# A first block convolved in pieces beside its own scans, inputs held whole, and a load of 97 rows split in two

## The chip, the cores and the metric

The kernel runs on one core of one Trainium2 chip. The metric is device time in microseconds: the median of several executions. Beside it stands one profiled execution, taken by the hardware profiler, with its own time and the span from its first to its last instruction. A core has five engines, each with its own queue of instructions that it works off in order: PE (TensorE, matmuls; PEld is its weight load), DVE (VectorE), ACT (ScalarE), POOL (GpSimd) and SP (SyncE), which here issues every DMA. Data lies in DRAM, in SBUF (on chip, up to 128 partitions) or in PSUM (where matmuls write).

## The reference

The program is a network of four layers on four images of 96 channels and 64x64 pixels, all in float32. Layers 0 and 1 are of concern here.

Layer 0 takes an image as a sequence of 4096 tokens and passes it twice through a Mamba block. Its core:

```
h  = layernorm(seq);  xs, z = split(h @ in_w)
xc = silu(depthwise conv of 4 taps over xs)
dt, B, C = split(xc @ xproj_w);  delta = softplus(dt @ dt_w + dt_b)
state[t] = exp(delta[t]*A) * state[t-1] + delta[t]*B[t]*xc[t]      # 16 states per channel
y  = sum over states of state*C + D*xc;   seq += (y*silu(z)) @ out_w
```

It ends in a 1x1 convolution and a batch norm over all four images (so nothing of the next layer can begin before the last image is done), and adds the input: `x0 = bn(out) + x`.

Layer 1 normalizes x0 in groups of three channels over the image, and passes it through two "ss2d" blocks, then adds x0 again. A block's core:

```
xa, z = split(x @ in_w);   xc = silu(depthwise conv 3x3 over xa)
for d in 4 directions (rows, columns, and both reversed):
    delta, B, C from tokens of xc in that direction;   scan as above, 8 states per channel
    ysum += y + D*xc, put back in row order
out = (layernorm(ysum) * silu(z)) @ out_w
```

Layers 2 and 3 (a Fourier mixer, attention and two feed-forward parts) follow and are not touched.

## The kernel before

The program has three stages, one after the other: `stage_mamba` (layer 0), `stage_ss2d` (layer 1) and `stage_tokens` (layers 2 and 3).

**How a scan is laid out.** Tokens are taken in turns of T=1024. For a turn the channels, spread over their states, fill the 128 partitions of a *unit*: 8 channels by 16 states in layer 0 (24 units a turn), 16 channels by 8 states in layer 1 (6 units a turn). The helper class `Scan` runs the units. For each it loads delta (`sc_d`, read from a DRAM copy `dd` so that each channel's row is repeated for its states), ACT makes exp(delta*A), DVE runs the scan (`TENSOR_TENSOR_SCAN`), POOL multiplies by C (`sc_h`), and PE sums over the states into `y`. For two units in three the input delta*x is spread by PE into PSUM (`s`) and multiplied by B on DVE; for the third it is loaded from DRAM (`sc_u`) and multiplied on POOL. Three units of layer 1 are reduced together, a *round*.

**What a turn needs first.** In layer 1 `Tokens.prepare` makes delta from xc by PE (`wdt`), ACT (bias, Softplus) and stores it as `dd`; `narrow` splits the B and C rows into bfloat16 parts (`bc_in`, `bc_part`, `bcd`, `bc_stack`), and `mix` spreads them over the partitions by PE (`selbc`) into `bc`.

**Blocks.** Layer 1 has eight blocks in the order image 0, image 1 (first pass), image 0, image 1 (second pass), then images 2 and 3 likewise. A block is 4 directions by 4 turns by 6 units, 96 units. `Block.prepare` runs `first_input` if it is a first pass, then the convolution (8 pieces of 8 rows, each 9 matmuls over the padded image `xp` into PSUM, an eviction on ACT into `xc`, and a Silu every 32 rows), then the gates (8 matmuls `w_in`, evicted into `ysum`, a Silu every 32 rows, stored to DRAM as `szd`). `ysum` later takes the sums of the scans. `xc` and `ysum` have two buffers each, so blocks alternate; `xp` has one. `first_input` loads the stage's input `mid` and the image `x` in pieces of 512 pixels into small buffers of a ring of two, scales `mid` by the batch norm (ACT), adds `x` (POOL), takes statistics (DVE) and stores the piece to DRAM as `x0d`; after the group statistics it loads every piece back from `x0d` and ACT writes it, scaled, into `xp`. `Block.finish` normalizes, multiplies by the gate and projects, into `xp` for the second pass, or adds `x0d` and stores.

**What sets the order.** Both scan stages are recorded first and placed afterwards. The class `Plan` records every operation with what it depends on; `Plan.order` then places them, each engine taking the earliest recorded operation that its own cost figures say is ready (the PSUM tiles named `mm`, two of them, are given out in the same pass). All of these have the line number of the one call that emits them, L467. What was recorded earlier goes first when both are ready. The order of recording is set by `Scan.run`: at each unit s it loads ahead (LOOK = 5 units), and lets `Work` objects take steps. A `Work` is a generator with a number of steps and a unit by which it is due; `pace` takes steps in proportion, `finish` takes the rest at once. `plan(s)` hands them in: the turn's `ready` (prepare), `narrowed` and `mixed`, and `between[n]` beside block n: the finish of block n-1 and the preparation of block n+1. Before the first unit, the first block's preparation is finished whole, turns 0 and 1 are prepared and narrowed, and turn 0 is mixed.

**The start of the first stage.** Before recording, `stage_mamba` loads its weights. `w_conv0`, the taps of the convolution, is 97 rows (96 channels and one for the bias of the norm) of 1536 numbers, repeated in each row. DVE multiplies it with the projection that PE has put in PSUM into `conv_w` (L799), copies the gate's part (`z_w`, L800), and so frees the two PSUM tiles that the first LayerNorm uses next.

Of the kernel before, what the change touches and what calls it, by code (L numbers as in the profile page):

```python
# [11 lines left out]
F32 = mybir.dt.float32  # L12
# [737 lines left out]
def stage_mamba(ctx: ExitStack, k: Common, x: bass.AP, mid: bass.AP, bn: bass.AP):  # L750
# [33 lines left out]
    dp_q = wp.tile([CP, 2, 64], F32, name="dp_q")  # L784
    with tc.tile_pool(name="m_ld", bufs=1) as ld:
        in_w = k.load(ld, "w_in0")
        taps = k.load(ld, "w_conv0")
        gl = ld.tile([C, C + 1], F32, name="gl")
        for i in range(2):
            nc.vector.tensor_scalar(dp_p[:, i, :], k.ident, vec("Dp", i, 0), None, ALU.mult)  # L790
            for h in range(2):
                g = slice(64 * h, 64 * h + 64)
                nc.vector.tensor_scalar(dp_q[g, i, :], k.ident[g, g], vec("Dp", i, 1)[g, :], None, ALU.mult)
            nc.vector.tensor_scalar(gl[:, 0:C], k.ident[:C, :C], k.vec("ln_g", i), None, ALU.mult)
            nc.vector.tensor_copy(gl[:, C:C + 1], k.vec("ln_b", i))
            pw = ps.tile([C + 1, 2 * DIN], F32, tag="mm", name="in_ps")
            nc.tensor.matmul(pw, gl, in_w[:, i, :], start=True, stop=True)
            for tap in range(4):
                nc.vector.tensor_tensor(conv_w[:, i, tap, :], pw[:, 0:DIN], taps[:, i, tap, :], ALU.mult)  # L799
            nc.vector.tensor_copy(z_w[:, i, :], pw[:, DIN:2 * DIN])  # L800
# [236 lines left out]
def stage_ss2d(ctx: ExitStack, k: Common, x: bass.AP, mid: bass.AP, bn: bass.AP, mid2: bass.AP):  # L1037
# [63 lines left out]
    class Block:  # L1101


        def __init__(self, b, i):
            self.b, self.i = b, i
            self.ready = None

        def first_input(self):

            b = self.b  # L1110
            st = wk.tile([C, L // W, 6], F32, tag="gn_st", name="gn_st", bufs=1)
            for t in range(L // W):
                cs = slice(t * W, (t + 1) * W)
                x0 = wk.tile([C, W], F32, tag="x0", name="x0")
                nc.sync.dma_start(out=x0, in_=mid[b, :, cs])
                xr = wk.tile([C, W], F32, tag="xr", name="xr")
                nc.sync.dma_start(out=xr, in_=x[b, :, cs])
                yield
                nc.scalar.activation(x0, x0, AF.Identity, scale=bn[:, 0:1], bias=bn[:, 1:2])
                nc.gpsimd.tensor_tensor(x0, x0, xr, ALU.add)  # L1120
                yield
                nc.vector.bn_stats(st[:, t, :], x0)
                nc.sync.dma_start(out=x0d[b, :, cs], in_=x0)
            mv = wk.tile([C, 2], F32, tag="gn_mv", name="gn_mv")
            nc.vector.bn_aggr(mv, st.rearrange("p a b -> p (a b)"))
            gm_ps = ps.tile([C, 1], F32, tag="mm", name="gm_ps")
            nc.tensor.matmul(gm_ps, group, mv[:, 0:1], start=True, stop=True)
            gm = wk.tile([C, 1], F32, tag="gm", name="gm")
            nc.vector.tensor_copy(gm, gm_ps)
            dm = wk.tile([C, 1], F32, tag="dm", name="dm")  # L1130
            nc.vector.tensor_tensor(dm, mv[:, 0:1], gm, ALU.subtract)
            gq = wk.tile([C, 1], F32, tag="gq", name="gq")
            nc.vector.scalar_tensor_tensor(gq, dm, dm, mv[:, 1:2], ALU.mult, ALU.add)
            yield
            gv_ps = ps.tile([C, 1], F32, tag="mm", name="gv_ps")
            nc.tensor.matmul(gv_ps, group, gq, start=True, stop=True)
            grs = k.rsqrt(wk, gv_ps, EPS, "gn_rs")
            yield
            shift = wk.tile([C, 1], F32, tag="gn_sh", name="gn_sh")
            nc.vector.scalar_tensor_tensor(shift, gm, -1.0, grs, ALU.mult, ALU.mult)  # L1140
            for t in range(L // W):
                x0 = wk.tile([C, W], F32, tag="x0", name="x0")
                nc.sync.dma_start(out=x0, in_=x0d[b, :, t * W:(t + 1) * W])
                yield
                nc.scalar.activation(
                    rows(8 * t, 8), x0.rearrange("p (h w) -> p h w", w=HW), AF.Identity, scale=grs, bias=shift
                )

        def prepare(self):
            i = self.i  # L1150
            if i == 0:
                yield from self.first_input()
            xc = self.xc = big.tile([C, L], F32, tag="xc", name="xc")
            for r in range(0, HW, 8):
                pa = ps.tile([C, W], F32, tag="mm", name="xc_ps")
                for tap in range(9):
                    nc.tensor.matmul(
                        pa, conv_w[:, i, tap, :], xp[:, r + tap // 3:r + tap // 3 + 8, tap % 3:tap % 3 + HW],
                        start=tap == 0, stop=tap == 8,
                    )  # L1160
                nc.scalar.activation(xc[:, r * HW:(r + 8) * HW], pa, AF.Identity, bias=k.vec("s_conv_b", i))
                yield 4
                if r % 32 == 24:
                    cs = slice((r - 24) * HW, (r + 8) * HW)
                    nc.scalar.activation(xc[:, cs], xc[:, cs], AF.Silu)

            ysum = self.ysum = big.tile([C, L], F32, tag="ysum", name="ysum")
            self.szd = dr.tile([C, L], F32, tag="szd", name="szd")
            for r in range(0, HW, 8):
                pz = ps.tile([C, W], F32, tag="mm", name="z_ps")  # L1170
                nc.tensor.matmul(pz, in_w[:, i, C:2 * C], rows(r, 8), start=True, stop=True)
                nc.scalar.copy(ysum[:, r * HW:(r + 8) * HW], pz)
                yield
                if r % 32 == 24:
                    cs = slice((r - 24) * HW, (r + 8) * HW)
                    nc.scalar.activation(ysum[:, cs], ysum[:, cs], AF.Silu)
                    nc.sync.dma_start(out=self.szd[:, cs], in_=ysum[:, cs])
# [24 lines left out]
    class Tokens(Turn):  # L1202
# [32 lines left out]
        def prepare(self):  # L1235

            i, d = self.block.i, self.d
            self.block.ready.finish()
            xt = self.xt = self.tokens()
            delta = wk.tile([CD, T], F32, tag="delta", name="delta", bufs=1)  # L1240
            for at in range(0, T, W):
                pd = ps.tile([CD, W], F32, tag="mm", name="dt_ps")
                nc.tensor.matmul(pd, wdt[:, i, d, :], xt[:, at:at + W], start=True, stop=True)
                bias = dt_b[:, i * NDIR + d:i * NDIR + d + 1]
                nc.scalar.activation(delta[:, at:at + W], pd, AF.Identity, bias=bias)
            nc.scalar.activation(delta[0:C, :], delta[0:C, :], AF.Softplus)
            dd = dr.tile([CD, T], F32, tag="dd", name="dd", bufs=2 + 2)
            nc.sync.dma_start(out=dd, in_=delta)
            yield
            du = wk.tile([C, T], F32, tag="du", name="du", bufs=2)  # L1250
            nc.gpsimd.tensor_tensor(du, delta[0:C, :], xt, ALU.mult)
            ud = dr.tile([C, T], F32, tag="ud", name="ud", bufs=2 + 1)

            nc.sync.dma_start(out=ud[64:C, :], in_=du[64:C, :])
            self.dd, self.du, self.ud = dd, du, ud
# [52 lines left out]
    for n in range(len(blocks)):  # L1308
        steps, count = [], 0
        if n > 0:  # L1310
            steps.append(blocks[n - 1].finish())
            count += 33
        if n + 1 < len(blocks):
            steps.append(blocks[n + 1].prepare())
            count += 9 + 8 * 4 + 26 * (1 - blocks[n + 1].i)
        between.append(Work(chain(*steps), count, (n + 1) * slot - 2 - 6 * 2))
        if n + 1 < len(blocks):
            blocks[n + 1].ready = between[-1]
    blocks[0].ready = Work(blocks[0].prepare(), 80, 0)

    def plan(s):
        out = []
        n, at = divmod(s, size)
        if at == 3 and 1 <= n + 1 < len(turns):
            turns[n + 1].mixed.due = s + 3
            out.append(turns[n + 1].mixed)
        if at == 5 and 2 <= n + 2 < len(turns):
            turns[n + 2].narrowed.due = s + 3
            out.append(turns[n + 2].narrowed)
        if at == 2 and 2 <= n + 2 < len(turns):  # L1330
            turns[n + 2].ready.due = s + 3
            out.append(turns[n + 2].ready)
        n, at = divmod(s, slot)
        if at == 6 and n < len(blocks):
            out.append(between[n])
        return out

    blocks[0].ready.finish()
    for turn in turns[0:2]:
        turn.ready.finish()  # L1340
        turn.narrowed.finish()
    turns[0].mixed.finish()
    sc.run(units, plan)
    for _ in blocks[-1].finish():
# [318 lines left out]
```

## Time and profile before

| | us |
|---|---|
| median of 3 runs | 7759.35 (7758.62 to 7760.86) |
| profiled execution, its own time | 7736.41 |
| its span | 7734.3 |
| PE busy | 6714.1 (87%) |
| DVE busy | 5775.7 (75%) |
| POOL busy | 5765.4 (75%) |
| ACT busy | 4616.8 (60%) |
| DMA queue of SP | 68.5% of 16 engines, 1368.76 MB |

The first stage lasts until about 2910 us, the second until about 6420, the third to the end. The busy shares are means over all three. A row of the windows gives the stretch, its length, then busy time and number of instructions of PE, PEld, DVE, ACT and POOL, the clock granted to PE as a share of full speed, the share of time that the 16 DMA engines were busy, and GB/s. A row of the timeline gives start, length, engine, line, operation, `out<-in` by the program's names with shapes and the number merged, and in brackets how long the engine had stood idle before and what ended that. A float32 matmul appears as two records, one for each pass. The profiled execution was 23 us shorter than the median of the runs.

### The profile page before, as it was taken

How to read it: one execution, taken by the hardware profiler on the slowest of the kernel's cores; microseconds unless marked ns; L12 is line 12 of the kernel's file. 1: busy time of each engine (PE TensorE's matmuls, PEld its weight loads, DVE VectorE, ACT ScalarE, POOL GpSimd, SP SyncE). 2: the span in 40 equal slices, each digit the busy share in tenths (PEclk: the TensorE clock that was granted, in tenths of full speed). 3: DMA queues.
4: the chain of work that ended last, by engine and by line, in shares of the span. 5: the costliest groups of instructions: out<-in, count | busy, mean ns of one | idle time of the engine just before them, and what ended most of it. 6: DMA issues, size and time to landing. Idle time of an engine off the chain costs nothing.

```text
span 7734.3 us, 84473 instructions
## 1 busy us (share of the span) xinstructions
PE 6714.1 (87%) x28872; PEld 2880.5 (37%) x28872; DVE 5775.7 (75%) x4491; ACT 4616.8 (60%) x6903; POOL 5765.4 (75%) x2836
## 2 busy tenths in 40 slices
PE   7988889888988877879898898889898877999997
PEld 2322233223323222223232322223232226888784
DVE  5989988988898882888888877788888873344343
ACT  4655555555555544767777766677777654445442
POOL 5989988989899882889898978789898971222323
PEclk9999999999999988889999897899899878889897
DMA  6988888988888874888888977788887862000000
GB/s 172 235 231 230 230 212 225 246 221 221 225 230 226 225 190 130 216 214 214 208 217 208 237 185 205 205 205 206 207 211 209 219 170 64 2 17 2 17 9 9
DMA packets 473180, 1374.15 MB, mean 178 GB/s; under 512 B 105678, under 2 KB 123807, under 8 KB 470700
## 3 DMA queue, kind: packets, MB, share of 16 engines
q1 hardware_dynamic: 472748, 1368.76, 68.5%
q8 instruction: 227, 3.72, 0.2%
q14 instruction: 205, 1.68, 0.1%
HBM read 1188.18 MB, written 180.36 MB: 177 GB/s over the span
## 4 chain that ended last, share of the span: by engine, by line
PE 53%; DVE 23%; issue 7%; ACT 6%; POOL 6%; DMA 5%; SPq 0%; DVEq 0%; POOLq 0%; ACTq 0%
PE mm L467 18%; PE s L467 14%; DVE sc_d L467 10%; DVE s L467 6%; PE y L467 5%; DVE sc_u L467 4%; POOL sc_h L467 3%; PE x_ps L1470 2%; DMA sc_d<-dd 2%; PE ln_rstd L544 2%; PE ln_cent L524 2%; PE ln_var L532 2%; PE zw_ps L1490 1%; DVE ysum L467 1%; PE h_ps L1442 1%
## 5 line engine op out<-in xcount | busy, mean ns | idle before, releaser
L467 POOL TENSOR_TENSOR sc_h<-sc_d,bc 128x1024 f32<-128x1024 f32 x1024 | 2407.0, 2357 | 375.5 <-DVE sc_d L467 255.9
L467 DVE TENSOR_TENSOR_SCAN sc_d<-sc_d,carry,s 128x1024 f32<-128x1024 f32 x768 | 1801.2, 2346 | 57.5 <-ACT sc_d L467 7.5
L467 DVE TENSOR_TENSOR s<-s,bc 128x1024 f32<-128x1024 f32 x1024 | 1249.3, 1220 | 503.7 <-PE s L467 339.5
L467 PE MATMUL s<-du,c_sel 96*128 96x512 f32 x2048 | 1170.7, 706 | 245.5 <-DVE sc_d L467 200.3
L467 ACT ACTIVATE sc_d<-sc_d,w_alog 128x1024 f32<-128x1024 f32 x1024 | 1166.8, 1146 | 308.5 <-DMA sc_d<-dd 304.7
L467 POOL TENSOR_TENSOR sc_u<-sc_u,bc 128x1024 f32<-128x1024 f32 x512 | 1207.1, 2358 | 191.8 <-ACT bc L467 117.1
L467 POOL TENSOR_TENSOR sc_h<-sc_u,bc 128x1024 f32<-128x1024 f32 x512 | 1207.2, 2358 | 118.0 <-PE y L467 100.7
L467 PE MATMUL y<-sc_h,c_red 128*32 128x512 f32 x6144 | 1072.4, 650 | 79.1 <-POOL sc_h L467 72.7
L467 DVE TENSOR_TENSOR_SCAN sc_u<-s,carry,sc_u 128x1024 f32<-128x1024 f32 x384 | 895.4, 2332 | 55.3 <-ACT s L467 38.9
L467 PE MATMUL s<-du,c_selp 128*128 128x512 f32 x1408 | 730.6, 648 | 112.4 <-DVE sc_d L467 109.3
L467 PEld LDWEIGHTS s<-du,c_sel 96*128 96x128 f32 x2048 | 419.4, 219 | 915.3 <-issue 464.6
L467 ACT ACTIVATE s<-sc_d,w_alog 128x1024 f32<-128x1024 f32 x512 | 570.6, 1115 | 193.5 <-DVE sc_d L467 117.7
L467 ACT ACT_TABLE_LOAD x492 | 631.2, 1283 | 12.9 <-DMA sc_d<-dd 4.3
L467 DVE TENSOR_TENSOR_SCAN sc_d<-sc_d,s 128x1024 f32<-128x1024 f32 x256 | 583.1, 2283 | 17.7 <-ACT sc_d L467 2.9
L509 POOL TENSOR_TENSOR ln_rs<-ln_rs_e,mhalf 128x4 f32<-128x4 f32 x128 | 134.5, 1052 | 566.7 <-DVE ln_rs_e L507 565.1
L467 PE MATMUL mm<-xp,w_conv 96*96 96x512 f32 x1152 | 523.0, 600 | 4.9 <-ACT bc L467 1.9
L467 PEld LDWEIGHTS y<-sc_h,c_red 128*32 128x32 f32 x6144 | 191.3, 113 | 790.9 <-issue 508.0
L467 PEld LDWEIGHTS s<-du,c_selp 128*128 128x128 f32 x1408 | 262.4, 201 | 540.4 <-issue 269.8
L467 ACT COPY carry<-sc_d 128x1 f32<-128x1 f32 x768 | 142.9, 186 | 478.7 <-DVE sc_d L467 470.2
L467 ACT COPY bc<-mm 128x512 f32<-128x512 f32 x512 | 282.8, 581 | 204.6 <-PE mm L467 199.9
L467 PE MATMUL mm<-hn,conv_w 97*64 97x512 f32 (+1 forms) x1024 | 368.3, 615 | 19.9 <-DVE hn L467 19.8
L467 DVE TENSOR_TENSOR_SCAN sc_u<-s,sc_u 128x1024 f32<-128x1024 f32 x128 | 290.7, 2271 | 25.2 <-ACT s L467 22.4
(211 smaller groups left out, 9436.0 us busy)
## 6 DMA issues: line engine op xcount, KB each, us to landing
sc_d<-dd SPq DMA_DIRECT2D x1536, 512.0 KB
sc_u<-ud SPq DMA_DIRECT2D x512, 512.0 KB
dd<-delta SPq DMA_DIRECT2D x128, 448.0 KB
bc<-bcd SPq DMA_DIRECT2D x64, 512.0 KB
ud<-du SPq DMA_DIRECT2D x192, 128.0 KB
dd<-delta SPq DMA_DIRECT2D x32, 512.0 KB
ud<-du SPq DMA_DIRECT2D x32, 512.0 KB
x<-x0d SPq DMA_DIRECT2D x64, 192.0 KB
```

The source lines that it names most:

```text
L467: getattr(getattr(self.nc, op.engine), method)(*a, **kw)
L509: nc.gpsimd.tensor_tensor(rs, ve, self.mhalf[:p, 0:n], ALU.pow)
L524: nc.tensor.matmul(mps, self.center_w, x[:, cs], start=True, stop=True)
L532: nc.tensor.matmul(vps[:, j:j + 1], sq[:, j * 128:(j + 1) * 128], self.mean_w, start=True, stop=True)
L544: nc.tensor.matmul(rps[:, j * 128:(j + 1) * 128], rs[:, q:q + 1].to_broadcast([128, C]), self.ident, start=True, stop=True,)
L1442: nc.tensor.matmul(ph[q * 64:(q + 1) * 64, j, :], xv[:, g * 4 + j, :], w1t[:, q * C:(q + 1) * C], start=True, stop=True,)
L1470: nc.tensor.matmul(px[:, j, :], fa[q][:, :, g * 4 + j], twid[:, g * 4 + j, :], start=True, stop=True)
L1490: nc.tensor.matmul(pw[:, j, :], zs[q][:, j, :], w2[:, q, :], start=q == 0, stop=q == 1)
```

## The change

Three edits, with what goes with them.

1. `w_conv0` is loaded by two DMAs, rows 0 to 95 and row 96.
2. `first_input` holds the image whole: `mid` goes into the block's `xc` and `x` into its `ysum`, in four pieces of 1024 pixels each, all loads recorded first; scaling, adding, statistics and the store to `x0d` go on in place in pieces of 512, and `xp` is written from there, so that `x0d` is not read back. A block of the second pass only takes the two buffers. `xp` is still in use by block 0 when image 1 comes to write it, so the rest of block 0's preparation is recorded ahead of that. The step counts of the `Work` objects follow (22 in place of 26).
3. `prepare` is split into `convolve(r0, r1)` and `gates`. The first block convolves 16 rows, makes its gates, and then convolves the other 48; its Silu is taken every 16 rows (in the others every 32). A turn's `prepare` no longer finishes the block's preparation, but steps it until the rows that it needs are there (a quarter of the image more for each turn of direction 0, all for the columns). Only turn 0 is prepared ahead; turn 1 joins the plan, and the first block's preparation is handed to the plan at the first look-ahead, due at unit 20.

```diff
-        taps = k.load(ld, "w_conv0")
+        taps = ld.tile([C + 1, 2, 4, DIN], F32, name="w_conv0")
+        for g in (slice(0, C), slice(C, C + 1)):
+            nc.sync.dma_start(out=taps[g], in_=k.w["w_conv0"][g])
...
         def first_input(self):
             b = self.b
+            x0 = self.xc = big.tile([C, L], F32, tag="xc", name="xc")
+            xr = self.ysum = big.tile([C, L], F32, tag="ysum", name="ysum")
             st = wk.tile([C, L // W, 6], F32, tag="gn_st", name="gn_st", bufs=1)
+            for t in range(L // T):
+                cs = slice(t * T, (t + 1) * T)
+                nc.sync.dma_start(out=x0[:, cs], in_=mid[b, :, cs])
+                nc.sync.dma_start(out=xr[:, cs], in_=x[b, :, cs])
+                yield
             for t in range(L // W):
                 cs = slice(t * W, (t + 1) * W)
-                x0 = wk.tile([C, W], F32, tag="x0", name="x0")
-                nc.sync.dma_start(out=x0, in_=mid[b, :, cs])
-                xr = wk.tile([C, W], F32, tag="xr", name="xr")
-                nc.sync.dma_start(out=xr, in_=x[b, :, cs])
+                nc.scalar.activation(x0[:, cs], x0[:, cs], AF.Identity, scale=bn[:, 0:1], bias=bn[:, 1:2])
+                nc.gpsimd.tensor_tensor(x0[:, cs], x0[:, cs], xr[:, cs], ALU.add)
                 yield
-                nc.scalar.activation(x0, x0, AF.Identity, scale=bn[:, 0:1], bias=bn[:, 1:2])
-                nc.gpsimd.tensor_tensor(x0, x0, xr, ALU.add)
-                yield
-                nc.vector.bn_stats(st[:, t, :], x0)
-                nc.sync.dma_start(out=x0d[b, :, cs], in_=x0)
+                nc.vector.bn_stats(st[:, t, :], x0[:, cs])
+                nc.sync.dma_start(out=x0d[b, :, cs], in_=x0[:, cs])
...
-            for t in range(L // W):
-                x0 = wk.tile([C, W], F32, tag="x0", name="x0")
-                nc.sync.dma_start(out=x0, in_=x0d[b, :, t * W:(t + 1) * W])
+            if self is not blocks[0]:
+                blocks[0].ready.finish()
+            xv = x0.rearrange("p (h w) -> p h w", w=HW)
+            for r in range(0, HW, 8):
+                nc.scalar.activation(rows(r, 8), xv[:, r:r + 8, :], AF.Identity, scale=grs, bias=shift)
                 yield
-                nc.scalar.activation(
-                    rows(8 * t, 8), x0.rearrange("p (h w) -> p h w", w=HW), AF.Identity, scale=grs, bias=shift
-                )
...
+            first = self is blocks[0]
+            yield from self.convolve(0, HW // 4 if first else HW)
+            yield from self.gates()
+            if first:
+                yield from self.convolve(HW // 4, HW)
...
+            run = HW // 4 if self is blocks[0] else HW // 2
...
-                if r % 32 == 24:
-                    cs = slice((r - 24) * HW, (r + 8) * HW)
+                if (r + 8) % run == 0:
+                    cs = slice((r + 8 - run) * HW, (r + 8) * HW)
                     nc.scalar.activation(xc[:, cs], xc[:, cs], AF.Silu)
+                    self.rows = r + 8
...
-            self.block.ready.finish()
+            rows = HW if d % 2 else (self.t + 1) * T // HW
+            while self.block.rows < rows:
+                self.block.ready.step()
...
-    blocks[0].ready = Work(blocks[0].prepare(), 80, 0)
+    blocks[0].ready = Work(blocks[0].prepare(), 22 + 8 * 4 + 9, 20)
...
-        if at == 5 and 2 <= n + 2 < len(turns):
+        if at == 5 and 1 <= n + 2 < len(turns):
...
-        if at == 2 and 2 <= n + 2 < len(turns):
+        if at == 2 and 1 <= n + 2 < len(turns):
...
+        if s == -sc.LOOK:
+            out.append(blocks[0].ready)
...
-    blocks[0].ready.finish()
-    for turn in turns[0:2]:
-        turn.ready.finish()
-        turn.narrowed.finish()
+    turns[0].ready.finish()
+    turns[0].narrowed.finish()
     turns[0].mixed.finish()
```

## The prediction

> **What bounds the kernel now.** No one engine does (PE 87% busy, DVE and POOL 75%), so I read where all stand still, in order: the chain of work that ended last, over the first 45 us; the windows between the two scan stages; the timeline there; windows over the eight blocks of layer 1.
>
> First 45 us: the chain in order of time (start, us, what), then DVE's timeline and one of the windows:
> ```profile
> 8.80 28.95 DMA w_conv<-in_w_conv_dram
> 37.77 1.15 DVE conv_w L799 x4
> ```
> ```profile
> 37.77 1.15 DVE L799 TENSOR_TENSOR conv_w<-mm,w_conv 97x192 f32<-97x192 f32 x4 [22.07 <-DMA w_conv<-in_w_conv_dram]
> ```
> ```profile
> 26.00:38.00 12.00, 0.00 (x0) 0.00 (x0) 0.23 (x1) 0.00 (x0) 0.00 (x0) 1.00 0.06 27
> ```
> The load of 97 rows takes 29 us. The last line (windows; final columns clock, DMA share, GB/s) shows 6% of sixteen DMA engines at 27 GB/s: one engine carries it. DVE waits, and all else behind DVE.
>
> Between the stages, windows, then timeline:
> ```profile
> 2910.00:2952.00 42.00, 5.02 (x20) 3.70 (x20) 15.16 (x47) 6.75 (x9) 14.34 (x10) 0.50 0.57 160
> 2952.00:3038.00 86.00, 78.39 (x168) 28.57 (x168) 6.73 (x14) 36.72 (x43) 10.82 (x10) 0.92 0.32 94
> 3038.00:3079.00 41.00, 40.58 (x87) 15.15 (x88) 1.16 (x4) 25.36 (x38) 4.43 (x2) 0.92 0.72 195
> ```
> ```profile
> 2952.36 0.81 ACT L467 ACTIVATE xp<-x,gn_sh,gn_rs 96x512 f32<-96x512 f32 x1 [5.78 <-DMA x<-x0d]
> 3037.68 0.30 SPq L467 DMA_DIRECT2D dd<-delta  x1
> 3050.98 17.33 PE L467 MATMUL mm<-xp,w_conv 96*96 96x512 f32 x40
> 3079.44 1.23 DVE L467 TENSOR_TENSOR s<-s,bc 128x1024 f32<-128x1024 f32 x1 [1.62 <-ACT bc L467]
> ```
> Columns: PE, weight loads, DVE, ACT, POOL, clock, DMA. Three stretches without a scan: 42 us for the first image's input (nobody busy), 86 us of PE alone, 41 us in which PE convolves image 1 while B and C of turn 0 wait behind it. Scans begin at 3079.4.
>
> Blocks, each cut where DVE starts its first sum into ysum:
> ```profile
> 3112.00:3499.00 387.00, 320.06 (x848) 98.60 (x847) 330.98 (x211) 274.90 (x419) 337.11 (x146) 0.84 0.84 214
> 3499.00:3895.00 396.00, 348.09 (x1086) 124.07 (x1085) 335.88 (x224) 301.45 (x461) 351.61 (x161) 0.94 0.83 212
> 4291.00:4739.00 448.00, 380.92 (x1094) 130.06 (x1093) 353.66 (x248) 310.70 (x467) 365.91 (x172) 0.88 0.82 210
> 4739.00:5193.00 454.00, 382.61 (x1092) 133.42 (x1090) 351.22 (x246) 308.25 (x467) 361.98 (x168) 0.87 0.79 204
> ```
> The third and fourth rows hold the inputs of images 2 and 3, and are 52 and 58 us longer than the second.
>
> **The skill.** "DMA: Bandwidth & Descriptors", "Why a DMA increments its semaphore by 16 and not by 1": the number of engines is the largest up to 16 that divides the slowest dimension; a 96-partition tile gets 16, 127 partitions one. 97 is prime, and the 27 GB/s agree. "TensorE: Matmul & The Clock Gate", "What's actually happening": an idle PE runs at half clock until some 3.4 us of work; here the clock is 0.50 up to 2957. Its "Architectural detail" says ACT and DVE are strictly first in, first out; so order decides, as at 3038-3079.
>
> The changed kernel's order of instructions on each engine is fixed when it is built, and can be read without running it; counts below are from it, durations from the trace of before.
>
> **A. The 97 rows.** 582 KB over 16 engines at the 223 to 325 GB/s of the windows 9 to 12 us is some 2.5 us. w_in, just ahead of it, was in use at 13.8, so w_conv lands near 16; the one row adds an issue (0.4 us). The products it scales end on PE at 15.4 and 17.4. DVE starts conv_w at 17 to 18 for 37.8: **-20** (18 to 22). Four seq loads behind it (1.57 MB, about 7 us) land by 23; DVE's BN_STATS on them stand ahead of ln_rs_e, due at 25. SP's four seq issues, which took 1.8 to 7.1 us each behind the slow load, get shorter. The order of the whole first stage is otherwise unchanged, so the gain is a shift of all that follows; were the two multiplications not first in DVE's queue, LayerNorm of seq would have hidden part of it.
>
> **B. First input.** Before, a two-buffer ring chains load, scale, add, store, next load: first load 2916.9, xp 2952.4, 35.5 us, with 3.5 us of reload at the end. After, eight loads of 384 KB (3.1 MB) go at once: 13 us at the 240 to 260 GB/s of 2912-2920, 2 us to land, ACT 0.8, POOL 1.3, DVE 0.7+0.4, group statistics 3.1 (2948.7 to 2951.8): xp at 2938, no reload. Image 1's eight loads now queue behind on SP, and ACT has three scalings of image 1 before xp: they need 4.3 MB landed, by 2937, so cost nothing; at 180 GB/s they would cost 6. **-14** (8 to 18).
>
> **C. To the first delta.** Before, xp to the store of dd took 85.3 us: 72 convolution matmuls at 0.86 (two passes of 0.43) are 62, eight gates 7, the rest waits for ACT, two wdt, table and Softplus. After, the order has 8 writes of xp on ACT (6.4), four gates fitted between and behind, 18 convolution matmuls (15.5), evictions and a Silu of 1024 (2.4), two wdt matmuls (1.7), two evictions, table, Softplus (3.7), plus some 5 us of cold clock and PSUM turns: 35. **-50** (42 to 54).
>
> **D. Delta to first scan.** Before, 41.8 us. After, PE has two gates, 27 convolution matmuls (23.2), wdt, s (5.1), two more before B and C: about 34 from dd. SP's second store of szd waits on the gates' Silu, with bc_in and eight scan loads queued behind: 2.5 us late, hidden by PE; uncovered it would be those 2.5. POOL's first du has seven adds of image 1 ahead, done by 2956. **-8** (0 to 12). Before, the same gap held some 25 us of image 1's convolution (58 passes at 0.43); now it holds the first block's own. First scan near 3007 (3079.4-14-50-8), A apart. Turn 1's delta and parts, finished ahead of the scans before, are now made in the first units; by its order ACT and PE reach them before unit 6 needs them.
>
> **E. What now runs beside scans.** Convolution matmuls after the first round: 33 before, 81 after. The 48 are 41 us of PE. A round (3 units) took 11.6 us and costs PE 7.2, so 4.4 are free; nine in the second round (7.7) overrun by some 4 to 5, the other 72 lie over sixteen rounds (177 us of PE in 186). But block 1, with 72 spread alike, took 25 us more than the last without any (371). I take **+15** (0 to 40). Two extra Silu with table loads (1.28 each) hide in ACT's 29% idle.
>
> **F. Images 2 and 3.** Removed: 8 reloads of 192 KB per image. Merged: 16 loads into 8. Per image the reload is 1.57 MB, 6 us of DMA, in a stretch (4360-4480) that moved 245 GB/s at 95%. In PE's order, block 3's convolutions stood 36, 9, 0, 18, 9 over five rounds: 100 us of PE for 58, the stall at 4496. After, 9, 9, 9, 0, 18, 9, 9, 9 over eight: 118 for 93. Block 4: excess 34 before, 13 after. So 42+34-26-13 = 37, plus 3 for DMA: **-40** (0 to -90). The cost: mid's four loads go as one burst of 1.57 MB (6 us) at the end of the previous block, ahead of scan loads; prefetched about five units, they absorb it; without that 6 us per image.
>
> Sum: -20-14-50-8+15-40 = **-117**. The profiled execution took 7736.4 (span 7734.3), so 7619; the median of the runs stands 23 higher, 7759.35, so **7642**.
>
> **Rivals.**
> Given back: E costs the whole 41, F nothing: -20-72+41 = -51, 7708. For it: PE runs at 94 to 100% in 3100-3200. Against: POOL and DVE set the pace over a block, not PE.
> More: F brings images 2 and 3 close to their neighbour (-85), E 5: -172, 7587. For it: traffic falls as well as piles. Against: the conv still takes eight rounds, not twelve.
> No effect on the scans: B and C of turn 0 wait for something in DMA order, the scan begins as before; A and B alone, -34, 7725. Against: between dd and first scan PE, not DMA, had work ahead of it.
> Slower: SP's queue. Stores of x0d for images 2 and 3 wait on POOL's adds with scan loads behind them; sixteen stores and two bursts. To lose, each of the sixteen must hold the scans 117/16 = 7.3 us plus its share of the rest; stores for images 0 and 1 waited 35.5 us in 16 on POOL before, 2.2 each. At 2.2 the loss is 35; it decides only above 7.3, giving 7759 and more.
>
> **Chances.** Forecast (7605 to 7685) 0.58; more 0.15; given back 0.17; no effect 0.05; slower or even 0.05. Range 7580 to 7715: it takes in the centres of the first three, and leaves out the last two and the tails, about 0.2 in all. Within 0.2% (15 us) is about what measurement cannot tell from no change. Faster 0.95, same 0.02, slower 0.03.
>
> **What would show it.** conv_w on DVE by 18 instead of 37.8; xp 34 us earlier (20 and 14); first scan some 92 us earlier; first block's span to its successor near 400; images 2 and 3's blocks near 425. Wrong if: seq loads hold ln_rs_e; ACT's scalings of image 1 hold xp; the first scan starts on time but the first block takes over 430; the blocks of images 2 and 3 stay at 450.

## The result and the profile after

The changed kernel takes 7670.9 us (median of 4 runs, 7659.45 to 7684.68) against 7758.99 us for the kernel before (4 runs, 7754.21 to 7760.86): ratio 0.9884 [0.9869, 0.9899], 88 us less (78 to 102). The forecast was 7642. The profiled execution took 7674.68 us, span 7672.9.

DVE's timeline of the changed kernel over the first 45 us (start, us, what, and in brackets the wait before it):
```profile
17.55 1.15 DVE L801 TENSOR_TENSOR conv_w<-mm,w_conv 97x192 f32<-97x192 f32 x4 [0.51 <-DMA w_conv<-in_w_conv_dram]
```
It stood at 37.77 before, behind a wait of 22 us; 0.5 us of that wait is left.

Windows of the changed kernel between the two scan stages (start:end, length; PE, weight loads, DVE, ACT, POOL busy; clock, DMA share, GB/s), then its timeline there:
```profile
2890.00:2920.00 30.00, 4.70 (x20) 3.63 (x20) 17.79 (x48) 9.35 (x13) 17.26 (x13) 0.50 0.97 237
2920.00:2955.00 35.00, 30.97 (x59) 10.45 (x60) 4.51 (x7) 22.43 (x31) 8.11 (x7) 0.83 0.48 147
2955.00:2989.00 34.00, 34.00 (x76) 12.34 (x74) 1.05 (x3) 20.24 (x24) 3.72 (x3) 0.95 0.71 190
```
```profile
2919.30 5.75 ACT L467 ACTIVATE xp<-xc,gn_sh,gn_rs 96x512 f32<-96x512 f32 x8 [2.02 <-DVE gn_sh L467]
2953.56 0.30 SPq L467 DMA_DIRECT2D dd<-delta  x1
2954.06 25.11 PE L467 MATMUL mm<-xp,w_conv 96*96 96x512 f32 x54 [1.73 <-ACT ysum L467]
2988.53 1.23 DVE L467 TENSOR_TENSOR s<-s,bc 128x1024 f32<-128x1024 f32 x1 [22.32 <-ACT bc L467]
```
The clock is 0.50 up to 2920 here too, with PE busy for only 4.7 of 30 us, and 0.83 in the next window, as "What's actually happening" in "TensorE: Matmul & The Clock Gate" of the Trainium skill has it for a PE that gets work. The input now fills the DMA engines (97% at 237 GB/s, 57% at 160 before), and its eight writes of xp follow one another without a reload. From xp to the first delta's store are 34 us instead of 85. Then PE convolves for 25 us (27 matmuls of two passes), with B and C of turn 0 behind them, and the first scan's multiply waits 22 us for these: 2988.5 instead of 3079.4.

Windows of the changed kernel over blocks 0 to 4 of layer 1 (counted from 0), each cut at its first sum into ysum:
```profile
3026.00:3422.00 396.00, 347.16 (x954) 110.14 (x952) 330.84 (x214) 295.36 (x442) 336.57 (x147) 0.88 0.82 207
3422.00:3827.00 405.00, 359.71 (x1091) 126.22 (x1090) 335.84 (x225) 301.35 (x460) 352.04 (x161) 0.92 0.83 208
3827.00:4244.00 417.00, 369.36 (x1093) 127.23 (x1093) 337.43 (x226) 305.93 (x468) 354.79 (x162) 0.89 0.82 207
4244.00:4679.00 435.00, 374.80 (x1086) 128.60 (x1085) 350.14 (x246) 310.20 (x465) 358.24 (x168) 0.87 0.81 208
4679.00:5110.00 431.00, 371.96 (x1090) 128.77 (x1088) 351.53 (x245) 303.68 (x460) 364.95 (x170) 0.91 0.82 211
```
Before, these were 387, 396, 396, 448 and 454. Images 2 and 3 (rows 4 and 5) gained, but rows 2 and 3, which the change does not seem to touch, lost 9 and 21. That is what the experiments had to explain.

### The profile page after: what moved, and what is told of

Same layout as the page of the kernel before. It is cut to its first block, busy times and chain, and to the rows that moved or that the text cites. A ratio compares the mean times of both kernels' runs of the same rounds, so it can differ in the third digit from the quotient of the medians.

```text
span 7672.9 us, 84380 instructions
## 1 busy us (share of the span) xinstructions
PE 6730.0 (88%) x28872; PEld 2894.6 (38%) x28872; DVE 5776.6 (75%) x4491; ACT 4628.9 (60%) x6911; POOL 5768.8 (75%) x2836
## 5 line engine op out<-in xcount | busy, mean ns | idle before, releaser
L467 PE MATMUL s<-du,c_sel 96*128 96x512 f32 x2048 | 1147.7, 693 | 214.8 <-DVE sc_d L467 186.3
L467 POOL TENSOR_TENSOR du<-delta,xc 96x1024 f32<-96x1024 f32 (+2 forms) x128 | 267.3, 2092 | 78.2 <-ACT delta L467 45.4
```

Of the source, the lines that this page charges most:

```text
L467: getattr(getattr(self.nc, op.engine), method)(*a, **kw)
```

## The experiments

One profile of each kernel, by the same cuts. "First" is the first sum into ysum; 0 to 6 are the blocks' lengths; "rest" is the last block and the last stage, whose code no kernel changes. All in us; the lengths are rounded from exact times, so they can differ by 1 from windows cut at whole us.

| kernel | first | 0 | 1 | 2 | 3 | 4 | 5 | 6 | rest |
|---|---|---|---|---|---|---|---|---|---|
| before | 3112 | 387 | 397 | 396 | 447 | 455 | 405 | 397 | 1739 |
| rows_only | 3088 | 386 | 398 | 399 | 454 | 454 | 407 | 400 | 1755 |
| after | 3026 | 396 | 405 | 417 | 435 | 431 | 410 | 397 | 1755 |
| after_again | 3020 | 392 | 412 | 414 | 435 | 433 | 417 | 394 | 1745 |
| rows_whole | 3046 | 392 | 408 | 404 | 428 | 433 | 418 | 402 | 1749 |
| rows_whole_2 | 3043 | 393 | 405 | 413 | 430 | 433 | 419 | 396 | 1745 |
| conv_whole | 3074 | 393 | 406 | 405 | 437 | 433 | 420 | 398 | 1747 |
| ring_23 | 3031 | 382 | 406 | 403 | 444 | 445 | 412 | 391 | 1748 |
| ring_23_2 | 3030 | 385 | 406 | 400 | 454 | 451 | 409 | 397 | 1759 |
| ring_held | 3025 | 385 | 404 | 399 | 457 | 453 | 415 | 395 | 1739 |
| mid_late | 3027 | 400 | 405 | 401 | 454 | 434 | 401 | 400 | 1750 |
| mid_paced | 3028 | 389 | 411 | 395 | 435 | 431 | 415 | 394 | 1759 |
| input_first | 3022 | 375 | 401 | 406 | 418 | 444 | 410 | 395 | 1756 |
| braided | 3029 | 375 | 398 | 411 | 416 | 444 | 399 | 392 | 1752 |

Every time below is a median with its ratio to the kernel before, run on the same chip. Intervals are about ±0.2%, 16 us, so differences of some 10 us are read from the table and only where several kernels agree.

**rows_only**: the kernel before with the split table alone.
```diff
-        taps = k.load(ld, "w_conv0")
+        taps = ld.tile([C + 1, 2, 4, DIN], F32, name="w_conv0")
+        for g in (slice(0, C), slice(C, C + 1)):
+            nc.sync.dma_start(out=taps[g], in_=k.w["w_conv0"][g])
```


> The kernel before, with the table of 97 rows loaded as 96 and 1 and nothing else. Forecast's term A: DVE multiplies the taps at 17.5 us instead of 37.8 and all behind it shifts by as much, so 20 us less than the kernel before (18 to 22), a ratio of 0.9974. Rival, LayerNorm or a later load takes over as the first stage's wait: 5 us less or nothing (0.9994 to 1.000), with the first write of xp less than 10 us earlier than 2952.4.

7734.6, ratio 0.9968 [0.9952, 0.9984]: 24 us less. In its trace conv_w is at 17.93, xp at 2930.66 (21.7 earlier), the first sum 23 earlier. The rival falls.

**rows_whole** and **rows_whole_2**: the reverse in the changed kernel, run twice, the second time beside the changed kernel itself (after_again, no edit).
```diff
-        taps = ld.tile([C + 1, 2, 4, DIN], F32, name="w_conv0")
-        for g in (slice(0, C), slice(C, C + 1)):
-            nc.sync.dma_start(out=taps[g], in_=k.w["w_conv0"][g])
+        taps = k.load(ld, "w_conv0")
```

> The changed kernel with its table of 97 rows loaded in one piece again. If the split is worth 20 us in the changed kernel too: about 7691 us, 20 above the changed kernel (ratio to the kernel before 0.9911). If what follows had absorbed the head start (images' input waiting for something else): 7671 to 7676.

> The changed kernel once more, beside the next three on one chip, as the measure for them. If its losses in blocks 1 and 2 (405 and 417 us, 396 and 396 before) and 19 us in the last stage, whose code is unchanged, were that execution's own: block 2 between 400 and 410, the last stage near 1375 us from the last sum into ysum (1389 in the first profile, 1370 in the kernel before).

> The changed kernel with its table of 97 rows loaded in one piece, now beside the changed kernel itself. If the split is worth its 20 us to the end: 17 to 23 us above it. If the head start is given back later: within 8 us of it, though the first sum into ysum comes 20 us later.

First time 7671.9, ratio 0.9887 [0.9866, 0.9908], no slower than the changed kernel on another chip, against the 7691 expected. Second time 7685.1, 0.9910 [0.9889, 0.9931], where the changed kernel beside it took 7665.6, 0.9886 [0.9864, 0.9908]: 19.5 us more. The traces agree with the second: the first sum is 20 and 23 us later, and the last sum, at 6307 and 6300 instead of 6284 and 6293, is 15 us later on average. The times alone, at this spread, do not settle it between 0 and 20; with rows_only and the traces I take 20.

after_again also answers what was the first profile's own. From the last sum to the end it took 1369 us, against 1389 in the first profile and 1371 before: that stage's 18 us were chance. Block 2 stays at 414, outside the 400 to 410 expected if its loss had been chance.

**conv_whole**: the changed kernel with its first block convolved before the scans.
```diff
-        first = self is blocks[0]
+        first = False
...
-            run = HW // 4 if self is blocks[0] else HW // 2
+            run = HW // 2
...
+    blocks[0].ready.finish()
     turns[0].ready.finish()
```


> The changed kernel, with the first block convolved whole before its gates and its first scans, as before; the held input and the split table stay. If the pieces are what moved the first sum (terms C, D, E: -50 -8 +15): about 43 us above the changed kernel, 7714 (ratio 0.9942), the first sum into ysum near 3080 instead of 3026, the first block back to 387, all blocks from the second on as in the changed kernel. Rival, the pieces are given back beside the scans (E 41): 20 us or less above the changed kernel, 7691 or below, first block under 375.

7715.6, ratio 0.9948 [0.9928, 0.9969], as expected to 2 us. Its first block, in the windows:
```profile
3074.00:3468.00 394.00, 324.63 (x841) 97.78 (x840) 330.84 (x212) 277.18 (x424) 335.36 (x146) 0.84 0.84 211
```
The first sum comes 51 us later than in the changed kernel (3074 against 3023, the mean of its two profiles). PE does 324.6 us in the block instead of 347.2, and the block is no shorter: 394 against 392 and 396. So the convolution that the changed kernel does beside its scans is hidden. The 7 us that its first block is longer than before are there without it too. Turn 1's delta, which conv_whole also prepares beside the scans, is not enough to explain them: the five kernels below with a ring for images 2 and 3 prepare it there as well, and their first blocks take 375 to 385. What the traces show to differ is the order in which the plan places block 0, on every engine, though its code is the same. Image 1's convolution, for one, lies over the rounds from round 7 on (counted from 0) as 7, 1, 6, 4, 2, 5, 5, 7, 6, 2, 9, 3, 6, 2, 7 in the changed kernel, and as 2, 4, 3, 4, 5, 4, 5, 9, 0, 9, 9, 0, 9, 0, 9 in these five. The six kernels with the first order have 389 to 400 in block 0 (mean 394), the five with the second 375 to 385 (mean 380). Why code for later images moves work in block 0 was not looked into.

**ring_23** and **ring_23_2**: images 2 and 3 come through the two-buffer ring and are reloaded, as before; images 0 and 1 held.
```diff
+            ring = b >= 2
+            if ring:
+                for t in range(L // W):
+                    x0 = wk.tile([C, W], F32, tag="x0", name="x0")
+                    nc.sync.dma_start(out=x0, in_=mid[b, :, cs])
...
+                    nc.sync.dma_start(out=x0, in_=x0d[b, :, t * W:(t + 1) * W])
```


> The changed kernel, with the first input of images 2 and 3 through the small ring and its reloads as before; images 0 and 1 held whole. Blocks 3 and 4 (counted from 0) go back from 435 and 431 to about 447 and 455. Theory 1, the held input also caused what blocks 1 and 2 lost (8 and 21 us, by the order in block 1 and by the burst of four loads of mid at the end of block 2): blocks 1 and 2 back at 396 and 396, and the time within 10 us of the changed kernel (7664 to 7684). Theory 2, those losses are of that execution or of the clock: blocks 1 and 2 stay at 405 and 417, and the kernel is some 36 us slower than the changed one, near 7707 (ratio 0.9933).

> The changed kernel with the first input of images 2 and 3 through the ring as before, now beside the changed kernel. If the held input of these two is worth the forecast's 40 us: 40 above the changed kernel. If blocks 3 and 4 gain some 34 and blocks 1, 2 and 5 give some 20 of it back: 5 to 20 above it. If it is worth nothing: within 5 us.

7665.0, 0.9873 [0.9849, 0.9897], and 7678.6, 0.9905 [0.9884, 0.9926], the second 13 us above the changed kernel beside it. Holding the two images is worth some 32 us in blocks 3 and 4 (897 for both on average, 861 to 870 with the held input and its burst), and next to nothing in the whole: by the ratios ring_23 is 8 us below the changed kernel, ring_23_2 beside it 13 us above. Block 2 goes back to 400 and 403, block 5 to 409 and 412, block 0 to 382 and 385. Block 1 does not, although every engine's order there is that of the kernel before: theory 1 holds for block 2 and not for block 1.

**mid_late** and **mid_paced**: the two attack the burst. In the changed kernel all of mid for image 2 is issued at once in the last four turns of block 2 (SP's timeline of the changed kernel):
```profile
4131.57 1.95 SPq L467 DMA_DIRECT2D xc<-mid  x4
```
mid_late makes each quarter wait for the ysum quarter that its x replaces; mid_paced for the first sum of the t-th turn of the block ahead.
First mid_late, in first_input, then mid_paced, whose early is called from the end of turn t of the block ahead; a copy of one column makes the load wait.
```diff
+                if b >= 2:
+                    nc.scalar.copy(x0[:, cs][:, 0:1], xr[:, cs][:, T - 1:T])
                 nc.sync.dma_start(out=x0[:, cs], in_=mid[b, :, cs])
```
```diff
+        def early(self, t, done):
...
+            nc.scalar.copy(self.xc[:, t * T:t * T + 1], done)
+            nc.sync.dma_start(out=self.xc[:, cs], in_=mid[self.b, :, cs])
...
+                    o.early(t, ysum[:, cs][:, 0:1])
```


> The changed kernel, but for images 2 and 3 each quarter of mid is loaded only once the quarter of ysum that its x goes into is finished, so that the four loads no longer go as one burst at the end of the block ahead. The order of the convolution in block 2 stays, in block 5 it becomes that of the kernel before. If the burst costs block 2 its loss: block 2 back from 404 to 417 to about 398, and 10 to 20 us less than the changed kernel. If the burst costs nothing: block 2 as in the changed kernel, time within 5 us of it. If the later loads come too late for the convolution: blocks 3 and 4 above 440.

> The changed kernel, but for images 2 and 3 mid's quarters are loaded one after each of the first four turns of the block ahead, instead of together at the end of the block before that. If the burst costs block 2 some 10 us: block 2 near 401, block 3 at 428 to 440, 5 to 15 us below the changed kernel. If loads that meet those of x and the stores in the block cost as much as the burst: block 3 near 450 and no gain.

mid_late: 7663.1, 0.9884 [0.9863, 0.9905], no gain. mid_paced: 7642.0, 0.9856 [0.9833, 0.9879], 22 us below the changed kernel by the ratios, with intervals that still overlap. Block 2 in the windows of after_again, then blocks 2 and 3 of mid_late and of mid_paced:
```profile
3823.00:4237.00 414.00, 366.69 (x1091) 126.19 (x1090) 337.38 (x226) 305.51 (x467) 354.35 (x162) 0.89 0.82 208
```
```profile
3832.00:4232.00 400.00, 359.47 (x1087) 126.03 (x1088) 336.07 (x224) 300.26 (x459) 352.38 (x161) 0.91 0.83 210
4232.00:4686.00 454.00, 389.42 (x1095) 137.17 (x1093) 351.03 (x247) 311.37 (x472) 364.08 (x170) 0.86 0.79 202
```
```profile
3828.00:4223.00 395.00, 350.35 (x1091) 123.45 (x1090) 336.37 (x226) 301.16 (x461) 352.93 (x162) 0.94 0.83 213
4223.00:4658.00 435.00, 380.92 (x1094) 132.29 (x1093) 346.63 (x247) 310.54 (x470) 365.28 (x171) 0.88 0.81 212
```
The convolution lies over the rounds of block 2 alike in all three. Five profiles with the burst have 404 to 417 there (mean 411); five without it (ring_23 twice, ring_held, mid_late, mid_paced), 395 to 403 (mean 399). Of these 11 us, 9 lie in the block's last four turns, where the burst is issued (mean 120.5 against 111.6); the other 2 lie ahead of it and are not its own. So the burst costs about 9 us, shown by taking it away in three ways. With it goes an order: in these four turns the plan places PE, ACT and SP otherwise than in the kernel before, and without the burst it places them as there. What is held is seen in DVE's waits of after_again and of mid_paced from 4113 to the end of block 2 (us in total, times, longest):
```profile
DVE ysum L467 <- PE y L467: 11.8, 2, 6.5
DVE s L467 <- ACT bc L467: 8.7, 2, 4.4
```
```profile
DVE s L467 <- ACT bc L467: 8.7, 2, 6.9
DVE ysum L467 <- PE y L467: 4.7, 1, 4.7
```
DVE's waits for PE's finished sums are 7 us longer with the burst; its own waits for B and C are the same. But POOL waits for B and C as well, and there the two differ. SP and POOL of after_again, then of mid_paced:
```profile
4136.73 0.36 SPq L467 DMA_DIRECT2D bc_stack<-bcd  x1
4151.10 2.35 POOL L467 TENSOR_TENSOR sc_u<-sc_u,bc 128x1024 f32<-128x1024 f32 x1 [10.66 <-ACT bc L467]
```
```profile
4128.21 0.31 SPq L467 DMA_DIRECT2D bc_stack<-bcd  x1
4140.02 2.37 POOL L467 TENSOR_TENSOR sc_u<-sc_u,bc 128x1024 f32<-128x1024 f32 x1
```
With the burst, SP has the load of the B and C parts behind stores and loads of delta, 8.5 us later, and POOL stands for 9 to 11 us at this place in all five profiles; in the five without the burst it does not. How much of the 9 us is the transfer itself and how much the order that the plan makes of it was not separated.

mid_late (second row of its fence) loses in block 3 what it won in block 2. All eight loads of image 2 then come beside the output work of block 2, which is the likely reason. mid_paced loads mid some 20 to 50 us earlier in the block, and keeps both gains.

**ring_held**: which half of the forecast's term F was it, the reloads or the ring? Pieces come through the ring, but are scaled into the block's own buffer and stay.
```diff
+                if b >= 2:
+                    m = wk.tile([C, W], F32, tag="x0", name="x0")
+                    nc.sync.dma_start(out=m, in_=mid[b, :, cs])
...
-                nc.scalar.activation(x0[:, cs], x0[:, cs], AF.Identity, scale=bn[:, 0:1], bias=bn[:, 1:2])
-                nc.gpsimd.tensor_tensor(x0[:, cs], x0[:, cs], xr[:, cs], ALU.add)
+                nc.scalar.activation(x0[:, cs], m, AF.Identity, scale=bn[:, 0:1], bias=bn[:, 1:2])
+                nc.gpsimd.tensor_tensor(x0[:, cs], x0[:, cs], r, ALU.add)
```


> The changed kernel; for images 2 and 3 the input comes in through the small ring as before, piece by piece, but is scaled and added into the block's own buffer, where it stays: no reload, and no burst. If the reloads are what blocks 3 and 4 lost before: blocks 3 and 4 below 440 (444 to 454 with ring and reloads, 428 to 435 in the changed kernel), blocks 0 and 2 as with the ring (382 to 385, 400 to 403), and the whole 15 to 25 us below the changed kernel, ratio near 0.9860. If the small ring is what holds them: blocks 3 and 4 stay above 440, time within 10 us of the changed kernel.

7676.5, 0.9896 [0.9873, 0.9920]. No reload, and the convolution in nine rounds of block 3's part (9, 0, 18, 9, 9, 9, 9, 0, 9 matmuls by PE's order, before 36, 9, 0, 18, 9); yet:
```profile
4213.00:4670.00 457.00, 387.23 (x1093) 133.37 (x1092) 356.12 (x247) 310.56 (x467) 363.34 (x169) 0.86 0.79 201
4670.00:5123.00 453.00, 393.01 (x1085) 133.06 (x1083) 349.35 (x246) 309.48 (x465) 360.43 (x169) 0.85 0.80 202
```
So neither the reloads nor the bunched convolution is what these blocks lost, unless ring_held brings a new cost of the same size; the one that the trace shows, a wait of 7.5 us (last section), is 5.3 us in ring_23 already.

**input_first** and **braided**: the ring with the held result, and the input ahead of the output work of the block two back, so that it starts earlier, with six of image 2's eight pieces of mid in the last four turns of block 2; braided also lets the convolution alternate with that output work.
First the edit of input_first to ring_held, then that of braided to input_first (braid takes one step of the convolution and three of the output work in turn).
```diff
+        if late:
+            steps.append(blocks[n + 1].first_input())
         if n > 0:
             steps.append(blocks[n - 1].finish())
```
```diff
+        if late and n > 0:
+            steps = [steps[0], braid(steps[1], steps[2])]
```


> As ring_held, and in the work between blocks the first input of images 2 and 3 goes ahead of the output work of the block two back, so that it need not wait for ysum. Its convolution then lies over fifteen rounds of the block instead of eight. If the bunched convolution is what keeps blocks 3 and 4 some 30 us above their neighbours: 405 to 420 each, and 25 to 50 us below the changed kernel, ratio 0.982 to 0.985. If DMA is what keeps them: they stay near 430.

> As input_first, and for images 2 and 3 the steps of the convolution alternate with the output work of the block two back instead of following it: no round has over 9 convolution matmuls of them (input_first: rounds of 15 and 18 in block 4, which took 444 us there, and none above 9 in block 3, which took 418). If the bunching sets these blocks: block 4 at 405 to 425, block 3 as in input_first, and 20 to 30 us below input_first, ratio near 0.980. If something else held block 4 (its loads): still above 435 and within 10 us of input_first.

input_first: 7627.9, 0.9835 [0.9811, 0.9860]; braided: 7623.4, 0.9835 [0.9814, 0.9856]. Both beat the kernel before and the changed one, some 38 us below the latter by the ratios, and the intervals stand clear of its 0.9869. Blocks 3 and 4 of input_first, then of braided:
```profile
4204.00:4621.00 417.00, 371.97 (x1097) 126.16 (x1096) 347.38 (x243) 307.64 (x466) 359.79 (x169) 0.90 0.86 219
4621.00:5065.00 444.00, 380.56 (x1094) 132.84 (x1093) 352.66 (x247) 307.63 (x464) 363.36 (x168) 0.88 0.79 201
```
```profile
4212.00:4629.00 417.00, 365.54 (x1110) 126.12 (x1110) 352.44 (x246) 313.49 (x473) 365.49 (x172) 0.92 0.87 221
4629.00:5072.00 443.00, 382.46 (x1084) 131.76 (x1082) 350.90 (x245) 300.80 (x457) 356.70 (x165) 0.86 0.79 200
```
braided has no round above 9 in block 4 (input_first 15 and 18), and block 4 is the same to 1 us: bunching falls a second time. So does DMA as a plain limit, since the DMA share is highest in the shorter block. Their gain lies in block 0 (375 instead of 394), in block 3, and by smaller amounts in 1, 2 and 5; block 4 is 12 us longer than in the changed kernel. Part of what block 3 gains is paid in block 2, whose last four turns take 120 and 119 us here, against 112 in the five kernels with neither burst nor early pieces. In block 0, 13 of the 19 us go with the other order (conv_whole); the rest is not settled. Its clock was 0.95 here, 0.88 to 0.90 in the changed kernel. Of block 4's 444 the traces show only where: in braided DVE waited 6.4 and 5.7 us in one turn for the chain of B and C.

## Why the prediction was right or wrong

The sum, with the means of the two profiles of the changed kernel against before and rows_only (whose blocks are those of the kernel before; the first sum is that of before):

| part | forecast | measured |
|---|---|---|
| A to D, to the first scan or sum | -92 | -91 (scan), -89 (sum) |
| E, block 0 | +15 | +7.5 |
| F, blocks 3 and 4 | -40 | -38 |
| blocks 1, 2 and 5 | 0 | +11, +18, +7.5 |
| block 6, the rest | 0 | -3, +3 |
| sum | -117 | -83 (by the times -88) |

**A, B, C, D right, term by term.** conv_w 20.2 earlier (-20); xp 33.1 earlier, so B is -12.9 (-14); the store of dd 84.1 earlier, so C is -51.0 (-50); the first scan 90.9 earlier, so D is -6.8 (-8). The loads of image 1 did not hold xp. conv_whole gives the worth of the pieces in the time: 45 us by the medians, 50 by the ratios. One count was low: between the store of dd and the first scan the trace of before has 68 passes of image 1's convolution, not 58, some 4 us more.

**E right in kind, too high in size.** The forecast let nine matmuls of the second round overrun and doubted that sixteen rounds hide the other 72. They do. Measured with and without the pieces: 394 and 393. By the trace, 30 matmuls stood behind the first round before, not 33, so that 51 were moved there and not 48. The 7.5 us that are left go with the order in which block 0 is placed: with the order of the ring kernels the block has the same pieces and takes 380, 6 us less than before. The rival in which this work gave the gain back is out.

**F right in its sum by luck, wrong in its reason.** Blocks 3 and 4 gave the 38. The excess of PE in bunched rounds (37) and the reloads (3) made up the forecast's 40, and the experiments speak against both: ring_held without reloads and with a looser order stays at 457 and 453, braided with an even order gains nothing over input_first. What the profiles leave is the way and the time in which the input comes: through a ring of two buffers behind the output work 444 to 457 in block 3, in whole quarters 428 to 437 (454 where mid comes late), through the ring ahead of the output work 416 to 418. With each way the plan also places every engine's work in these blocks in another order, so the order is not ruled out as the cause. By which wait it acts was not settled.

**The step that failed** is the price of F's burst: "prefetched about five units, they absorb it; without that 6 us per image". They do not: image 2's burst costs block 2 about 9 us, and with it the chain of B and C comes some 8 us later in SP's queue. With it the forecast took blocks that the change does not touch as unchanged, and they were not. In block 5, the changed kernel's order spreads the next block's convolution from round 7 on (6, 3, 0, 1, 7, 1, 4, 5, 1, 8, 0, 9, 9, 9, 9) instead of from round 10 (4, 5, 0, 9, 0, 9, 9, 9, 0, 9, 9, 9). The seven profiles with the first order have 410 to 420 (mean 416), the six with the second 401 to 412 (mean 407): 9 us that go with the order (braided has a third, and 399). It was there to be read before the run. Block 1's 11 us are open for the greater part. Its order is at most some 5 of them: the six kernels with the changed kernel's order have 405 to 412 (mean 408), the five that hold the first images but have the order of the kernel before have 398 to 406 (mean 403), against 397 and 398 before. So of the 36 us by which blocks 1, 2 and 5 missed the forecast, the burst and the orders of blocks 5 and 1 go with some 22; no run changed an order alone.

## What to carry to other kernels

A transfer that nothing waits for still costs what it delays: load a prefetch one piece at a time and early enough (mid_paced against mid_late), and price a burst by what stands behind it in the queue, here the chain of B and C. Where a scheduler orders the work, compare the orders of all stages and not only of the changed one, since a changed buffer moves work in blocks that the diff does not name. And when a sum comes out right, test its terms: here 38 us came as forecast, and two experiments spoke against the cause that was given.

## What was not expected of the hardware

A DVE operation on 96 elements, 0.16 us where nothing held it, lasted up to 7.5 us. In ring_held, DVE's timeline and then POOL's:
```profile
4399.25 7.50 DVE L467 SCALAR_TENSOR_TENSOR gn_sh<-gm,gn_rs 96x1 f32<-96x1 f32 x1
```
```profile
4396.95 0.55 POOL L467 TENSOR_TENSOR gn_rs<-gn_rs_e,mhalf 96x1 f32<-96x1 f32 x1 [2.65 <-DVE gn_rs_e L467]
4397.48 4.66 POOL L467 TENSOR_TENSOR sc_h<-sc_d,bc 128x1024 f32<-128x1024 f32 x2
4402.10 2.34 POOL L467 TENSOR_TENSOR sc_h<-sc_u,bc 128x1024 f32<-128x1024 f32 x1
4404.39 2.34 POOL L467 TENSOR_TENSOR sc_u<-sc_u,bc 128x1024 f32<-128x1024 f32 x1
```
It ends at 4406.75, POOL's run of four multiplies at 4406.73. The Trainium skill, "SBUF — State Buffer", "SBUF: two separate sides", says that DVE with two inputs in SBUF and GpSimd take a shared pair of ports by an exclusive lock for a whole instruction, if the one on GpSimd (POOL) reads SBUF. The trace agrees, and adds that DVE did not get in between four instructions that followed one another. The statistics of an image sit on DVE's queue ahead of the scans, so each such wait holds the scans.

PE's clock differed between executions with the same work. In block 1, in the same order, PE's 1086 to 1091 recorded matmuls took 348 us at a granted clock of 0.94 (before) and 361.3 at 0.91 (ring_23), and the block 396 and 406. Which way the cause runs, a lower clock or waits that let it drop, the profiles do not say.
